# A second seven-product level in layer 3's second matrix, and layer 0's row vector fetched from DRAM, in a four-layer graph kernel on one core

## The chip, the core and the metric

The kernel runs on one core of one Trainium2 chip, in one launch. The metric is the device time in microseconds (us) of that launch; the figure of the kernel before is the median of three runs. All data are 32-bit floats. In the profile PE is TensorE's multiplying side and PEld its weight loads, DVE is VectorE, ACT is ScalarE, POOL is GpSimd, and SP is the engine whose queue issues nearly all DMA transfers. One matrix multiplication of the program shows in the profile as two weight loads and two MATMUL records (a transposition shows as one of each).

## The reference, cut to what matters

There are 128 graphs of 64 nodes with 512 features: `x` is 128x64x512, `adj` is 128x64x64. Four layers follow each other, each of the form x = layernorm(x + layer(x)). Layer 0 and layer 3 are what the change touches:

```python
# layer 0
s = (x @ w) @ a
A = tanh((s[..., :, None] + s[..., None, :]) / 8.0) * 8.0
A = exp(where(A >= 0, A, 0.1 * A)) * adj
A = A / sum(A, axis=-1) * sum(adj, axis=-1)
out = A @ x @ w
# layer 3: x 512 wide, W1 1024x512, W2 512x1024; H = (adj != 0)
h = layer_norm(relu(hypergraph_conv(x, adj, W1, b1)), gamma, beta)
y = hypergraph_conv(h, adj, W2, b2) + x
# hypergraph_conv(x, adj, W, b) = Dn * (H @ (Be * (H.T @ (x @ W.T)))) + b
```

Layer 1 has three 512x512 matrices (two of them are multiplied together beforehand), layer 2 likewise.

## The kernel before, in words

**Tiling.** Two graphs share the 128 partitions, which makes 64 tiles of 128 tokens. A group is two tiles (`GT` = 2, `TOK` = 256 tokens), so there are 32 groups; two groups (`SG` = 2) are a pair and go through the layers together. The first and the last pair (`APART_3A`) are the exception: their four groups run one by one. So 14 calls of `run` handle a pair and 4 handle a single group. `run` records every layer's operations for its groups.

**Seven products.** Every large matrix is applied by a seven-product scheme: the left side is cut into 2x2 blocks ("11" to "22") with four sums of them (`side_sums`), the matrix into four blocks and three combinations (`combine`), and seven products of blocks replace eight. `pair_products` does this for a pair (512 tokens). The seven matrix pieces come from DRAM: `stored_in_place` and `stored_twice` store them once at the start, and `streamed` loads them for each call into the eight buffers of kind "ring", 512 KB a load (1024 floats a partition).

**Layer 3's first matrix ("3a")** already goes one level further for pairs: `forty_nine_products` treats each of the seven products as seven again. `inner_sums` makes four sums on DVE for the left side, `inner_products` issues seven products into two PSUM banks, and `into` carries them out of PSUM, three steps on ACT and three on DVE for each of the seven sets. DVE (and twice POOL) then adds the seven results in `use`.

**Layer 3's second matrix ("3b")** before is one level: `pair_products(a, s_, streamed("3b"), ..., chunks=KH // 2)`. That is 7 products x 2 token halves x 4 chunks, 56 multiplications of 128x128 by 128x256 for a pair. Each product is added into `x` by DVE straight from PSUM with the node scale (`pair_scaled_into`), 14 instructions for a pair.

**Layer 0's row vector.** `row_dot` makes s for a tile as a column, one value a partition. Tanh needs it as rows as well: ACT writes the column times an identity (`diag`), and `over_graph(diag, ps_s)` multiplies that with the block matrix of ones `same` on PE, so that s stands in PSUM along the free axis in all partitions of its graph; ACT reads it from there. `over_graph` is used twice more for each group, for row sums in layers 0 and 2.

**What sets the order.** `run` executes nothing itself: each step adds operations to `Order`, with the engine, a planned cost (`w_pe`, `w_dve`, `w_act`, `w_pool`) and a key. `Order.run` lists them by planned times, gives out buffers (`kinds`: 17 "k4", 8 "ring", 7 "x" and so on) and emits them; every engine then keeps that order strictly. Keys come from the fitted tables `BASE` (one number for each group), `EARLY`, `LEAD` and `PREPARED`. PE has "whole" operations (all 128x128 cells) and divided ones ("quarters" and "columns", which use 64 rows or columns and run side by side); `choose` plans a cost (`TURN`) for going from one to the other. `over_graph` may be either. DVE operations that read no PSUM, and all of POOL's, are marked `port` and planned so that they do not overlap.

Of the kernel before, what the change touches and what calls it, by code (L numbers as in the profile page):

```python
# [16 lines left out]
P = 128  # L17
B, N, D, DH = 128, 64, 512, 1024
T = B * N // P
GT = 2  # L20
# [8 lines left out]
APART = 4  # L29

BASE = [
    6.0035, 8.2772, 13.2033, 17.6332, 26.0202, 27.1146, 41.4888, 43.61,
    52.2405, 53.0756, 62.4617, 70.5981, 77.7498, 79.4232, 91.2587, 95.4559,
    102.4733, 106.2595, 111.4315, 119.1324, 126.0769, 128.4967, 140.1767, 144.9507,
    152.9702, 154.7354, 165.7456, 173.1973, 169.6391, 182.4004, 188.4128, 191.0087,
]
RESIDENT = ("m1", "m2")
APART_3A = (0, NG // SG - 1)
LEAD = [37.2697, 5.5754]
PREPARED = [28.6382, 16.68, 12.9121, 14.55, 17.8769, 0.587]  # L40
PIECE = 1024
EPS = 1e-5
TINY = 1.1754944e-38
# [26 lines left out]
class Order:  # L70
    LATENCY = {"PE": 210, "DVE": 125, "ACT": 140, "POOL": 120, "SP": 3500}
    AGAIN = {"PE": 0, "DVE": 115, "ACT": 115, "POOL": 120}
    TO_PE = 50
    BYTES_PER_NS = 260
    UNDERWAY = 8
    TURN, TURN_DIVIDED = 110, 60

    NEAR = 27.7595
    FAR = 251.4563
    ENOUGH = 0.0205  # L80

    EARLY = [14.4537, -21.4408, 7.6077, 25.6747, 2.625, 1.3768, 16.3015, 8.7929, -1.7454, 13.9409, 11.8891, -1.629, 2.9263, -2.9931, 14.9219, -6.7676]

    BLOCK = 64
    REST = 4500
    AHEAD = 15.591
    TOGETHER = 0.0013
    OLDEST = 1000000000.0
    SPARE = {"k4": 0, "ring": 1}

    def __init__(self, slots):
        self.slots = {kind: list(range(n))[::-1] for kind, n in slots.items()}
# [204 lines left out]
def kernel(  # L297
# [34 lines left out]
    def kind(name, n, *shape, space=None):  # L332
        kinds[name] = [(space or sbuf).tile([P, *shape], FP, name=f"{name}{i}") for i in range(n)]

    kind("x", 7, GT, D)
    kind("k4", 17, PIECE)
    kind("ring", 8, PIECE)
    kind("h", 2, GT, DH)
    kind("k2", 2, D)
    kind("adj", 6, CT, N)  # L340
    kind("kept", 6, CT, N)
    kind("bh", 2, CT, N + 2)
    kind("e", 4, GT, N)
    kind("col", 28, 16)
    kind("bank", 8, D, space=psum)
    kinds["product"] = [None] * 3
# [357 lines left out]
                made[f"b{h + 1}{i + 1}"] = (q, lambda q=q: rows_of(q, cols // 2))  # L704
        return made

    def stored_twice(which, w):

        stored_in_place(which + "1", quarters(w), PIECE, PIECE)
        width = w.shape[1] // 4  # L710
        store = in_dram(which, width, [k + "." + j for k in USE for j in USE])
        for n, (k, (src, _)) in enumerate(zip(USE, stored[which + "1"])):
            order.key = PREPARED[4] + PREPARED[5] * n
            q = Buf("k4", 4)
            order.add("SP", 500, [src, in_turn], [q], lambda q=q, src=src: nc.sync.dma_start(out=q.t, in_=src.t), size=P * PIECE * 4)
            view = lambda q=q: rows_of(q, 2 * width)
            b = {f"b{h + 1}{i + 1}": (q[2 * h + i], lambda view=view, h=h, i=i: view()[:, h : h + 1, ts(1 - i, width)])
                 for h in range(2) for i in range(2)}
            for j in USE:
                if j[0] == "b":  # L720
                    store(k + "." + j, b[j])
            t = {"t1": b["b11"], "t3": b["b12"], "t2": b["b22"], "t4": b["b21"]}
            combine(b, t, width)
            for j in USE:
                if j[0] == "t":
                    store(k + "." + j, t[j])

    order.key = PREPARED[2]
    stored_twice("3a", w3a)


    order.key = PREPARED[3]
# [9 lines left out]
    for k, (q, view) in w3b_q.items():  # L742
        for c in range(KH // 2):
            row = (int(k[1]) - 1) * (KH // 2) + c
            act(D // 2, [gamma_c, q], [q], lambda view=view, c=c, row=row: nc.scalar.activation(
                view()[:, c, :], view()[:, c, :], AF.Identity, scale=gamma_c.t[:, row : row + 1]))
    stored_in_place("3b", w3b_q, PIECE, PIECE)

    def streamed(which, room=()):

        pieces = []
        chunks = {"3a": 1, "3b": KH // 2}.get(which, KC // 2)
        for src, n in stored[which]:
            width = PIECE // src.cells
            t_ = Buf("ring")
            order.add("SP", 500, [src[list(range(n))]], [t_, *(room if not pieces else ())],
                      lambda t_=t_, src=src, n=n, width=width: nc.sync.dma_start(
                          out=t_.t[:, : n * width], in_=src.t[:, : n * width]),
                      urgent=1.5, size=P * n * width * 4)
            if pieces:  # L760
                order.ops[-1].led = lead
            else:
                lead = order.ops[-1]
            for k in range(n):
                pieces.append((t_, lambda t_=t_, k=k, width=width: t_.t[:, ts(k, width)].rearrange(
                    "p (c o) -> p c o", c=chunks)))
        return pieces
# [294 lines left out]
        return room, at  # L1062


    def inner_products(raw, room, at, which, pieces, f, width):


        going, x_, y_ = Buf("inner"), Buf("bank"), Buf("bank")
        raw_tok, raw_view = raw

        def side(k):
            if k in KEYS:
                return raw_tok, lambda: raw_view(k)
            return room[int(k)], lambda: at(int(k))[:, which]

        def times(bank, i, k, start=True):
            piece, view = next(pieces)
            token, left = side(k)

            def emit():  # L1080
                nc.tensor.matmul(bank.t[:, ts(i, width)], left(), view()[:, 0], start=start, stop=True, skip_group_check=True)

            pe(w_pe(width), [token, piece, going], [bank, *([y_] if k == "11" else [])], emit, matmuls=1)

        def into(cells, bank, i, n=1, first=False):
            n *= width
            dst = lambda: f.t[:, cells[0] * width : cells[0] * width + n]
            src = lambda: bank.t[:, i * width : i * width + n]
            if first:
                act(n, [bank], [f[cells]], lambda: nc.scalar.copy(dst(), src()), NOW)  # L1090
            else:
                dve(n, [bank, f[cells]], [f[cells]], lambda: nc.vector.tensor_add(dst(), src(), dst()), NOW)

        times(x_, 1, "11")
        times(x_, 0, "0", False)
        into([1, 2], x_, 0, 2, True)
        times(y_, 0, "12")
        times(x_, 1, "1", False)
        times(x_, 0, "3", False)
        into([0], x_, 1, 1, True)  # L1100
        into([0], x_, 0)
        into([2], y_, 0)
        times(x_, 1, "2", False)
        into([1], x_, 1)
        times(x_, 1, "22", False)
        into([3], x_, 1, 1, True)
# [198 lines left out]
    def run(groups):  # L1305
# [27 lines left out]
        for g in groups:  # L1333
            step(0, g)
            xt, own = xt_[g], own_[g]
            adj, turned, gm, am, sums, g1, dc, dh = prepared[g // GC]
            s, diag, e, ps_s = Buf("col", GT), Buf("e", GT), Buf("e", GT), Buf("bank")
            for t in range(GT):
                row_dot([xt[[2 * t, 2 * t + 1]], u0_b], s[t], lambda t=t, xt=xt: xt.t[:, t, :], lambda: u0_b.t)
                act(N + 40, [s[t]], [diag[t]], lambda t=t, s=s, diag=diag: nc.scalar.activation(  # L1340
                    diag.t[:, t], eye, AF.Identity, scale=s.t[:, t : t + 1]))

            over_graph(diag, ps_s)
            for t in range(GT):
                act(N + 40, [ps_s, s[t]], [e[t]], lambda t=t, s=s, e=e, ps_s=ps_s: nc.scalar.activation(
                    e.t[:, t], tiles(ps_s)[:, t], AF.Tanh, bias=s.t[:, t : t + 1]), NOW)
            dve(GT * N, [e], [e], lambda e=e: nc.vector.scalar_tensor_tensor(e.t, e.t, 0.1, e.t, ALU.mult, ALU.max))
            act(GT * N, [e], [e], lambda e=e: nc.scalar.activation(e.t, e.t, AF.Exp, scale=8.0))
            dve(GT * N, [e, adj], [e], lambda e=e, adj=adj, own=own: nc.vector.tensor_mul(e.t, e.t, adj.t[:, own]))

            ps_e, rs = Buf("bank"), Buf("e")
            over_graph(e, ps_e)
            dve(7 * GT * N, [ps_e], [rs], lambda rs=rs, ps_e=ps_e: nc.vector.reciprocal(flat(rs.t), ps_e.t[:, : GT * N]), NOW)
            dve(GT * N, [e, rs], [e], lambda e=e, rs=rs: nc.vector.tensor_mul(e.t, e.t, rs.t))
            step(1, g)
            gT0.append(gathered(*of_x[g], lambda h, t, e=e: e.t[halves[h][0], t, :], [e]))
            scales.append((sums, 2 * CT + own.start))
# [204 lines left out]
        step(15)  # L1562
        sx = {g: Buf("col", 2 * GT) for g in groups}
        if n == SG:
            pair_products(a, s_, streamed("3b"), *pair_scaled_into([xt_[g] for g in groups], scales, [sx[g] for g in groups]), chunks=KH // 2)
        else:
            g, (f, at) = groups[0], scales[0]
            seven_products({**a, "deep": True}, s_, streamed("3b"), *scaled_into(at_x[g], f, slice(at, at + GT), D // 2, sx[g]))
        for g in groups:
            step(15, g if n == 1 else last_of)  # L1570
            xt = xt_[g]
# [101 lines left out]
```

## Time and profile before

| | |
|---|---|
| median of three runs | 2114.53 us (2114.24 to 2114.62) |
| the profiled execution's own time | 2114.4 us |
| its span, first to last instruction | 2112.6 us |
| granted TensorE clock | 0.999 |
| PE / PEld busy | 2097.3 (99%) / 1773.1 us (84%) |
| DVE busy | 1361.7 us (64%), 3768 instructions |
| ACT busy | 1168.2 us (55%), 2538 instructions |
| POOL busy | 458.3 us (22%), 434 instructions |
| DMA | 345.00 MB, mean 163 GB/s |

The span leaves out 1.8 us of the execution's own time. Nearly every instruction has one line number (L1602 before, L1654 after), that of the function that records the emitted instruction, so groups are told apart by the names of the buffers: `bank<-ring,k` is a multiplication into a PSUM bank with one operand from a "ring" buffer (a streamed matrix piece) and one from a "k" buffer. A group line ends with the busy time, the mean duration of one in ns, and the idle time of the engine just before these instructions with what ended it. MATMUL records overlap each other (a new one starts while the last one drains), so their mean duration is not what one costs; the distance from start to start is.

### The profile page before, as it was taken

How to read it: one execution, taken by the hardware profiler on the slowest of the kernel's cores; microseconds unless marked ns; L12 is line 12 of the kernel's file. 1: busy time of each engine (PE TensorE's matmuls, PEld its weight loads, DVE VectorE, ACT ScalarE, POOL GpSimd, SP SyncE). 2: the span in 40 equal slices, each digit the busy share in tenths (PEclk: the TensorE clock that was granted, in tenths of full speed). 3: DMA queues.
4: the chain of work that ended last, by engine and by line, in shares of the span. 5: the costliest groups of instructions: out<-in, count | busy, mean ns of one | idle time of the engine just before them, and what ended most of it. 6: DMA issues, size and time to landing. Idle time of an engine off the chain costs nothing.

```text
span 2112.6 us, 49594 instructions
## 1 busy us (share of the span) xinstructions
PE 2097.3 (99%) x19867; PEld 1773.1 (84%) x19867; DVE 1361.7 (64%) x3768; ACT 1168.2 (55%) x2538; POOL 458.3 (22%) x434
## 2 busy tenths in 40 slices
PE   8999999999999999999999999999999999999998
PEld 4887788888888888888888888888888888888876
DVE  5765668765677547676585664866667665675644
ACT  3445655663555546664555664647447465374555
POOL 1121230411214013130131311222121221222120
PEclk9999999999999999999999999999999999999999
DMA  8677674533436236262352533435434454253655
GB/s 293 214 259 260 242 239 153 188 139 123 143 120 223 80 113 208 94 223 102 113 179 92 198 121 106 165 123 183 140 103 156 137 191 140 80 186 120 208 175 200
DMA packets 142102, 345.00 MB, mean 163 GB/s; under 512 B 32240, under 2 KB 49840, under 8 KB 141872
## 3 DMA queue, kind: packets, MB, share of 16 engines
q1 hardware_dynamic: 141872, 341.83, 47.4%
q8 instruction: 157, 2.57, 0.5%
q14 instruction: 73, 0.60, 0.1%
HBM read 305.70 MB, written 36.08 MB: 162 GB/s over the span
## 4 chain that ended last, share of the span: by engine, by line
PE 98%; ACT 1%; DMA 0%; DVE 0%; issue 0%; SPq 0%; POOL 0%; POOLq 0%; ACTq 0%; DVEq 0%
PE bank L1602 98%; ACT k L1602 1%; DMA k<-in_wk_dram 0%; DVE e L1602 0%; ACT x L1602 0%; SPq L1602 0%; ACT e L1602 0%; ACT m L1602 0%; DVE col L1602 0%; DVE k L1602 0%; POOL col L1602 0%; DVE m L1602 0%; POOLq L1669 0%; DVE x L1602 0%; ACT bw_b L1602 0%
## 5 line engine op out<-in xcount | busy, mean ns | idle before, releaser
L1602 PE MATMUL bank<-ring,k 128*128 128x256 f32 (+1 forms) x4940 | 1178.3, 387 | 0.3 <-ACT k L1602 0.3
L1602 PEld LDWEIGHTS bank<-ring,k 128*128 128x128 f32 x4940 | 916.8, 190 | 146.8 <-issue 24.5
L1602 ACT COPY k<-bank 128x512 f32<-128x512 f32 (+1 forms) x822 | 406.7, 529 | 368.0 <-PE bank L1602 365.0
L1602 DVE SCALAR_TENSOR_TENSOR x<-bank,col,x 128x256 f32<-128x256 f32 (+1 forms) x736 | 341.3, 503 | 218.6 <-PE bank L1602 204.8
L1602 PE MATMUL bank<-k,m 128*128 128x256 f32 (+1 forms) x2016 | 426.7, 358 | 0.7 <-ACT k L1602 0.7
L1602 PEld LDWEIGHTS bank<-k,m 128*128 128x128 f32 x2016 | 347.4, 190 | 43.9 <-issue 1.9
L1602 POOL TENSOR_TENSOR col<-col,mhalf 128x2 f32<-128x2 f32 (+1 forms) x161 | 111.8, 695 | 1007.0 <-DVE col L1602 750.9
L1602 DVE TENSOR_TENSOR k<-bank,k 128x256 f32<-128x256 f32 (+1 forms) x456 | 216.2, 494 | 158.4 <-PE bank L1602 107.4
L1602 ACT ACTIVATE k<-x,col 128x512 f32<-128x512 f32 x256 | 183.6, 720 | 187.8 <-DVE col L1602 160.7
L1602 PE MATMUL bank<-ring,h 128*128 128x256 f32 x1024 | 238.2, 380 | 0.0
L1602 ACT ACTIVATE x<-x,col,col 128x512 f32<-128x512 f32 x256 | 199.0, 814 | 53.1 <-DVE col L1602 52.9
L1602 PEld LDWEIGHTS bank<-ring,h 128*128 128x128 f32 x1024 | 192.7, 190 | 27.1 <-issue 0.9
L1602 DVE TENSOR_TENSOR k<-k,k 128x512 f32<-128x512 f32 (+3 forms) x319 | 191.6, 617 | 4.0 <-ACT k L1602 3.7
L1602 DVE TENSOR_TENSOR k<-k 128x256 f32<-128x256 f32 (+2 forms) x223 | 113.9, 526 | 61.7 <-ACT k L1602 53.5
L1602 DVE TENSOR_SCALAR col<-col 128x2 f32<-128x2 f32 (+2 forms) x402 | 73.8, 193 | 86.2 <-ACT k L1602 75.2
L1602 DVE TENSOR_TENSOR h<-k,k 128x1024 f32<-128x1024 f32 (+1 forms) x88 | 105.7, 1208 | 18.3 <-ACT k L1602 18.1
L1602 POOL TENSOR_TENSOR k<-k,k 128x1024 f32<-128x1024 f32 (+1 forms) x31 | 72.1, 2326 | 182.0 <-DVE h L1602 65.9
L1602 PE MATMUL bank<-k,k 128*64 128x64 f32 (+1 forms) x2112 | 104.1, 237 | 5.5 <-DMA k<-in_wk_dram 5.5
L1602 POOL TENSOR_TENSOR k<-k,b3b_b 128x512 f32<-128x512 f32 x64 | 82.3, 1293 | 116.3 <-ACT k L1602 51.7
L1602 PEld LDWEIGHTS bank<-k,k 128*64 128x64 f32 (+1 forms) x2112 | 77.0, 139 | 33.8 <-issue 20.4
L1602 POOL TENSOR_TENSOR x<-x,bv_b 128x512 f32<-128x512 f32 x64 | 81.3, 1279 | 106.2 <-ACT k L1602 34.2
L1602 ACT ACTIVATE k<-bank,u_c 128x256 f32<-128x256 f32 (+1 forms) x144 | 59.9, 445 | 65.2 <-PE bank L1602 65.1
(103 smaller groups left out, 1624.4 us busy)
## 6 DMA issues: line engine op xcount, KB each, us to landing
ring<-3a SPq DMA_DIRECT2D x196, 512.0 KB, 4.3
ring<-3b SPq DMA_DIRECT2D x126, 512.0 KB, 4.3
ring<-v SPq DMA_DIRECT2D x105, 512.0 KB, 4.4
ring<-w SPq DMA_DIRECT2D x51, 512.0 KB, 4.9
x<-in_x_dram SPq DMA_DIRECT2D x32, 512.0 KB, 5.2
out_dram<-x SPq DMA_DIRECT2D x31, 512.0 KB, 4.7
ring<-v SPq DMA_DIRECT2D x35, 256.0 KB, 4.4
3a<-k SPq DMA_DIRECT2D x49, 128.0 KB, 3.8
```

What stands on the lines that cost most here:

```text
L1602: made = f(*args, **kwargs)
```

## The change

1. **3b for pairs becomes 49 products.** `run` calls `inner_sums` and `inner_products` for each of the seven outer products, with two chunks each (`parts=2`) and a result width of 128 columns: 7 x 7 x 2 = 98 multiplications of 128x128 by 128x128. Seven sets of results go to SBUF buffers of kind "k2", are added there (`sum_of`, five times on DVE and twice on POOL for a pair), and reach `x` by 8 DVE instructions that now read SBUF (`into_x`).
2. **Its pieces.** `stored_twice` becomes `stored_inner`, called for "3a" as before and for "3b" too: seven stored pieces are loaded again, combined (21 DVE and 7 POOL instructions in all) and stored as 49 pieces of 128 KB. A pair streams 13 loads (6.4 MB) where it streamed seven (3.7 MB). The four single groups keep the seven pieces, now called "3b1".
3. **s as rows.** For groups from the third on, `diag` and its `over_graph` go. The column is stored to DRAM (one DMA of 4-byte elements) and loaded back as rows, once for each half of the partitions; tanh reads SBUF. The first two groups keep the old way.
4. **Tables and buffers.** `BASE`, `LEAD`, `PREPARED`, `EARLY` and the planner's constants get other values; "x" goes from 7 buffers to 6, "k4" from 17 to 15, "bh" from 2 to 1, "k2" from 2 to 8 and "e" from 4 to 6. So the whole list of every engine is ordered anew.

```diff
-    TO_PE = 50
-    BYTES_PER_NS = 260
-    UNDERWAY = 8
+    TO_PE = 100
+    BYTES_PER_NS = 290
+    UNDERWAY = 6
...
-    stored_in_place("3b", w3b_q, PIECE, PIECE)
+    stored_in_place("3b1", w3b_q, PIECE, PIECE)
+    stored_inner("3b", D // 4, 2, PREPARED[3] + PREPARED[6], PREPARED[5])
...
-    def inner_products(raw, room, at, which, pieces, f, width):
+    def inner_products(raw, room, at, which, pieces, f, width, parts=1):
...
             def emit():
-                nc.tensor.matmul(bank.t[:, ts(i, width)], left(), view()[:, 0], start=start, stop=True, skip_group_check=True)
-
-            pe(w_pe(width), [token, piece, going], [bank, *([y_] if k == "11" else [])], emit, matmuls=1)
+                for c in range(parts):
+                    nc.tensor.matmul(bank.t[:, ts(i, width)], left() if parts == 1 else left()[:, c], view()[:, c],
+                                     start=start and c == 0, stop=c == parts - 1, skip_group_check=True)
+
+            pe(w_pe(width, parts), [token, piece, going], [bank, *([y_] if k == "11" else [])], emit, matmuls=parts)
...
-                act(N + 40, [s[t]], [diag[t]], lambda t=t, s=s, diag=diag: nc.scalar.activation(
-                    diag.t[:, t], eye, AF.Identity, scale=s.t[:, t : t + 1]))
-
-            over_graph(diag, ps_s)
+            if g < SG:
...
+                over_graph(diag, s_row)
+                rows_of_s = lambda s_row=s_row: tiles(s_row)
+            else:
+                s_row, kept_s = Buf("e", 2), const(dram.tile([GT * P], FP, name=f"s_{g}"))
+                dma(P * 64, [s], [kept_s], lambda kept_s=kept_s: kept_s.t.rearrange("(t p) -> p t", p=P), lambda s=s: s.t[:, :GT])
+                for h, (rows, _) in enumerate(halves):
+                    src = kept_s.t.rearrange("(t h i) -> h t i", h=2, i=N)[h]
+                    dma(P * GT * N * 2, [kept_s], [s_row[h]], lambda rows=rows, s_row=s_row: s_row.t[rows],
+                        lambda src=src: bass.AP(tensor=src.tensor, offset=src.offset, ap=[[0, N], *src.ap]))
...
-            pair_products(a, s_, streamed("3b"), *pair_scaled_into([xt_[g] for g in groups], scales, [sx[g] for g in groups]), chunks=KH // 2)
+            outer_of = {"1": a["11"], "2": a["12"], "4": a["22"], "5": s_[0], "6": s_[1], "7": s_[2], "3": s_[3]}
+            pieces, kept_3b = iter(streamed("3b")), {}
...
+            for name in ("1", "5", "2", "6", "3", "7", "4"):
+                token, view = outer_of[name]
+                blocks = {k: (lambda k=k, view=view: view()[:, ts(col(k), 2), ts(row(k), P)]) for k in KEYS}
+                room, at_room = inner_sums({"tokens": token, **blocks}, (P, 2))
+                f = Buf("k2", 4)
+                inner_products((token, lambda k, blocks=blocks: blocks[k]()), room, at_room, 0, pieces, f, P, 2)
+                if name == "2":
+                    into_x(0, 0, sum_of(kept_3b["1"], f, out=f))
...
+                elif name == "4":
+                    into_x(1, 0, sum_of(kept_3b["7"], f, out=f))
+                kept_3b[name] = f
```

## The prediction

> **What bounds the kernel now.** I read the page's busy line first, then the chain that ended last.
>
> ```profile
> PE 2097.3 (99%) x19867; PEld 1773.1 (84%) x19867; DVE 1361.7 (64%) x3768; ACT 1168.2 (55%) x2538; POOL 458.3 (22%) x434
> PE 98%; ACT 1%; DMA 0%; DVE 0%; issue 0%; SPq 0%; POOL 0%; POOLq 0%; ACTq 0%; DVEq 0%
> ```
>
> PE never rests, and the chain is PE itself. So the time is the sum of the distances from one matmul's start to the next. The timeline of PE gives them: subtract the start of a row from that of the next and divide by its count.
>
> ```profile
> 59.24 1.95 PE L1602 MATMUL bank<-k,m 128*128 128x128 f32 x16
> 61.02 3.62 PE L1602 MATMUL bank<-ring,k 128*128 128x256 f32 x16
> 64.48 0.49 PE L1602 MATMUL bank<-e,same 128*128 128x128 f32 x2
> ```
>
> A record 128 columns wide costs 1.78/16 = 0.111 us, one of 256 costs 3.46/16 = 0.216 us. Half the columns cost 51%. The third view is the timeline where PE goes from whole to divided operations and back.
>
> ```profile
> 348.71 1.89 PE L1602 MATMUL bank<-ring,k 128*128 128x256 f32 x8
> 350.53 1.63 PE L1602 MATMUL bank<-kept,h 64*64 64x64 f32 x96
> 352.08 3.72 PE L1602 MATMUL bank<-ring,k 128*128 128x256 f32 x16
> 355.74 0.69 PE L1602 MATMUL bank<-kept,h 64*64 64x64 f32 x32
> 356.25 1.11 PE L1602 MATMUL bank<-e,x 64*64 64x64 f32 x64
> ...
> 2092.73 0.69 PE L1602 MATMUL bank<-kept,h 64*64 64x64 f32 x32
> 2093.36 1.99 PE L1602 MATMUL bank<-ring,k 128*128 128x256 f32 x8
> ```
>
> The x8 row takes 1.82 us, 0.09 over 8 x 0.216, because a divided row follows; the x16 row takes 3.66, 0.20 over, because it stands between two. The 32 divided records take 0.51 us when divided ones follow and 0.63 when a whole one does. One excursion into divided work thus costs 0.09 + 0.11 + 0.12 = 0.32 us beside the work itself.
>
> The last view, groups kept apart by shape, has the prices for the other engines; the stretch line shows their load in the steady part, with PE unbroken.
>
> ```profile
> L1602 DVE SCALAR_TENSOR_TENSOR x<-bank,col,x 128x256 f32<-128x256 f32 x672 | 297.0, 480 | 201.7 <-PE bank L1602 188.2 <-ACT k L1602 5.5 <-POOL k L1602 2.7
> L1602 DVE TENSOR_TENSOR k<-k,k 128x512 f32<-128x512 f32 x169 | 119.5, 729 | 3.9 <-ACT k L1602 3.7
> L1602 DVE TENSOR_TENSOR k<-k 128x256 f32<-128x256 f32 x137 | 58.1, 443 | 22.1 <-ACT k L1602 18.1 <-POOL k L1602 2.3 <-PE bank L1602 1.4
> L1602 DVE TENSOR_TENSOR k<-k,k 128x256 f32<-128x256 f32 x116 | 56.8, 498 | 0.1
> L1602 DVE DVE_READ_ACCUMULATOR x<-bank,col,x 128x1 f32 x448 | 37.0, 83 | 0.0
> L1602 DVE TENSOR_TENSOR e<-bank,kept 128x128 f32<-128x128 f32 x32 | 9.3, 289 | 20.3 <-PE bank L1602 19.4 <-ACT h L1602 0.5
> 264.00:1980.00 1716.00, 1716.00 (x16425) 1476.69 (x16425) 1122.19 (x3100) 962.78 (x2088) 380.15 (x353) 1.00 0.43 147
> ```
>
> **The change part by part.** The sum is made against the profiled execution: 2114.4 us, of which 2112.6 are span; the median, 2114.53, stands 0.1 above it, which I ignore.
>
> *3b on PE.* A pair loses 56 multiplications of 256 columns, 112 records, 24.2 us, and gets 98 of 128 columns, 196 records, 21.8 us. Over 14 pairs: 338.7 - 304.6 = **34.1 us saved**. All of it lies on the path. Lower bound: at 0.112, which a run of 11 such records nearby shows, 31.4.
>
> A rule of the Trainium skill speaks against this step. The page "TensorE: Matmul & The Clock Gate", section "Back-to-back issue gap", says that in a stream where every matmul has its own weight load the spacing is set by both, and gives about 81 ns for 128 columns where the matmul alone would need 56, a factor of 1.45. By that the 2744 new records would cost 137 us more and the change would be a loss of about 100 us. The x16 row is such a stream, each record with its own 128-column load, and shows no such surcharge; I go by the row.
>
> *s as rows on PE.* By the emitted order 31 whole `over_graph` calls go: 62 records x 0.111 = **6.9 us saved**; ACT loses 60 diagonals of 0.34 us.
>
> *The new order on PE.* Counting the runs in the emitted lists, PE enters divided work 165 times before and 197 times after, with the same divided work. 32 x 0.32 = **10.2 us lost**. Bounds: 32 x 0.20 (the whole side alone) = 6.4, and 12.
>
> *DVE.* A pair gets 28 block sums of 256 (0.45 each, the mean of the two 256 rows), 21 additions of 128 from PSUM (0.29), five of 512 (0.71) and eight scaled additions of 256 with accumulator (0.44 + 0.08): 12.6 + 6.1 + 3.5 + 4.2 = 26.4 us. It loses 14 scaled additions, eight with accumulator: 6.8 us. Times 14, and 21 preparation instructions of 0.45: +284 us, to 1646 us, 79% of the new span. ACT gets 42 us net of copies by 98 sets x (0.37 + 2 x 0.27) = 89 less 20: about 1237 us, 59%. POOL gets 28 additions of 512 at 1.28 and 7 of 0.73: +41, to 499 us. None of this is on the path as long as PE has other work. But PE now waits inside each set: the products go in two banks, and the fourth, sixth and seventh product need ACT's and DVE's removal first. Before, seven sets a pair had three such round trips; now fourteen have, and on DVE whatever is queued ahead (a 1024-wide addition takes 1.2 us) delays all later PSUM removals, and with them PE. In the steady part of before DVE idles 35% and PE waits nowhere (1716.00 of 1716.00); afterwards DVE idles 21%. Bounds for new waits: 0, and, were 3b's DVE work confined to 3b's own PE time, (26.4 - 21.8) x 14 = 64 us. By the emitted order 3b's products come mostly in runs of 2 to 16 with other stages' work between them, so I am near the low end: **8 us lost**.
>
> *DMA and SP.* Pairs stream 38.5 MB more, preparation reads 3.7 and writes 6.4 MB more: 345 to about 394 MB, 189 GB/s; the page's slices reach 293. SP issues 1076 transfers for 847, about 0.4 us each, hidden. The store of s and the two loads wait on SP for `row_dot` and for the store's landing, and behind them queue the ring loads. The nearest rows, loads of rows from DRAM (`adj<-mask_rows`, 4.5 us to landing) and the store `mask_rows<-e` (4.4), make the way 9 us where ACT, PE and ACT took about 1. That is hidden by the rest of a pair's 131 us; uncovered it would cost up to 8 us a pair, 112 in all. I take 0.
>
> *The end.* Before, the last group's normalization is split by tile: from the last PE end (2105.9) to the end of the span pass 6.7 us, with two stores of 256 KB landing in 2.0. In the emitted order after, group 30 ends last, unsplit: scaled addition 0.56, column work 0.31, two squares with accumulators 1.82, column work and POOL's power 1.02, two scalings 1.6, about 0.6 of handovers, and a store of 512 KB, 0.4 to issue and between 2.0 and 4.4 to land. 8.3 to 10.7 us, so **3 us lost**. The start keeps its order of loads: 0.
>
> Sum: -34.1 - 6.9 + 10.2 + 8 + 3 = -19.8; 2114.4 - 19.8 = 2094.6, forecast **2095 us**.
>
> **Rivals.** What separates no change from a change here is 0.2%, 4.2 us: faster is below 2110.3, slower above 2118.8.
>
> *No new waits.* Excursions at 6.4 and no waits: 2114.4 - 34.1 - 6.9 + 6.4 + 1.6 = 2081. For it: PE waits nowhere in the steady part. Against: DVE's idle share falls by two fifths.
>
> *DVE becomes the bound inside 3b.* Without waits the sum is 2086.6; it is slower than before from 32 us of waits on, half of the 64. For it: DVE's work for a set, 26.4/7 = 3.8 us, exceeds PE's 3.1, and the 3a sets before them are dense too. With 45 us of waits: 2132. Against: the interleaving in the emitted order, and that 79% leaves room over a pair.
>
> *The saving is just eaten.* Waits of 24 to 32 us, by the same mechanism or by the ring loads coming late behind the s transfers: 2114.
>
> **How the numbers follow.** Forecast case (waits of 2 to 24 us) 0.62, no new waits 0.15, just eaten 0.07, DVE-bound 0.16. Faster 0.77, same 0.07, slower 0.16. The range goes from 2078 (the no-wait case with 128-column records at 0.110) to 2124, which leaves out the worse half of the slower case.
>
> **What the profile after would show.** `bank<-ring,k` and `bank<-ring,h` groups of 128x128, 2744 records together, in timeline runs of 0.111 us each; a pitch near 0.16 would break the first step. `bank<-e,same` falls by about 60 records. DVE near 1650 us. In the waits of PE, DVE `k` and ACT `k` should sum to a few us, in the stretches in mid-run PE should stay over 99%; if DVE's row there is over 90% while PE's is under 97%, the DVE rival holds. PE waiting for `ring<-3b` would mean late loads. The last store would be a single 512 KB one, some 9 us after the last matmul.

## The result, and the profile after

The changed kernel takes 2245.8 us (median of four runs, 2239.0 to 2248.8) against 2114.51 for the kernel before in the same session: a ratio of 1.0616, with a 95% interval from 1.0596 to 1.0637. It is 131 us slower, and the range of the forecast ended at 2124. The profiled execution took 2245.1 us, of which 2243.2 are span.

The page's busy line and the chain that ended last, by engine and by line:

```profile
PE 2125.0 (95%) x20985; PEld 1804.4 (80%) x20985; DVE 1554.5 (69%) x4460; ACT 1230.7 (55%) x2772; POOL 501.7 (22%) x469
PE 61%; DMA 10%; ACT 4%; DVE 3%; issue 1%; SPq 1%; POOL 0%; ACTq 0%; POOLq 0%; DVEq 0%
PE bank L1654 61%; DMA s<-col 5%; DMA e<-s 4%; ACT k L1654 2%; DVE k L1654 2%; DVE h L1654 1%; ACT h L1654 1%; DMA ring<-3a 1%; DMA ring<-3b 1%; SPq L1654 1%; ACT x L1654 1%; ACT e L1654 0%; DVE col L1654 0%; DVE x L1654 0%; POOL col L1654 0%
```

PE was 98% of the chain and is 61%. Two transfers that did not exist before, the store of s (`s<-col`) and its loads as rows (`e<-s`), hold 8.2% (4.5 and 3.7 before rounding). The steady stretch (columns: window, us, busy time and count for PE, PEld, DVE, ACT and POOL, granted clock, DMA share, GB/s) says how far PE is from unbroken work:

```profile
264.00:1990.00 1726.00, 1639.85 (x16457) 1414.29 (x16456) 1230.07 (x3505) 966.38 (x2172) 404.90 (x371) 0.98 0.51 163
```

86 us of the 1726 are without PE, and DVE is at 71%, less loaded than forecast. The list of waits (total us, times, longest) tells for whom PE stands, and who stands for s. `DVE e` is the end of the chain that starts with s: tanh and exp on ACT, then DVE, then PE.

```profile
SPq L1654 <- DMA s<-col: 161.9, 27, 8.4
ACT e L1654 <- DMA e<-s: 105.0, 24, 12.9
PE bank L1654 <- ACT k L1654: 32.5, 22, 5.2
PE bank L1654 <- DVE e L1654: 26.0, 10, 8.5
```

SP, which issues nearly all transfers, stands 161.9 us for the landing of `s<-col`, with everything queued behind. The DMA issue lists (count, KB each, median us to landing) give what the forecast had taken as 4.4 and 4.5:

```profile
s<-col SPq DMA_DIRECT2D x30, 1.0 KB, 8.2
e<-s SPq DMA_DIRECT2D x60, 32.0 KB, 3.5
```

The smallest transfer of the kernel, 1 KB, takes longer to land than any other that recurs through it (`x` follows with 5.7). One place shows the damage, first in the chain (start, us, what), then in the timeline of PE:

```profile
567.41 8.33 DMA s<-col
576.51 10.43 DMA e<-s
```

```profile
579.38 1.03 PE L1654 MATMUL bank<-k,m 128*128 128x256 f32 x4
588.90 0.80 PE L1654 MATMUL bank<-e,same 128*128 128x128 f32 x2 [8.49 <-DVE e L1654]
589.49 1.91 PE L1654 MATMUL bank<-ring,k 128*128 128x256 f32 x4
591.20 3.73 PE L1654 MATMUL bank<-k,m 128*128 128x256 f32 x12
```

From the issue of the store to the landing of the rows it takes 19.5 us (567.41 to 586.94). PE runs out of work at 580.4 and stands 8.5 us, the last two of them after the rows have landed, with ACT and DVE between them and PE. Afterwards four records of 256 columns take 1.71 us, 0.43 each, twice the 0.216 of before. The stretches around it show both reasons (the pair's second store went out at 577.2):

```profile
580.00:588.00 8.00, 0.41 (x2) 0.01 (x1) 0.37 (x3) 0.99 (x4) 0.00 (x0) 0.68 0.97 61
588.00:592.00 4.00, 3.10 (x8) 2.62 (x9) 1.91 (x8) 3.19 (x10) 0.70 (x1) 0.50 0.25 91
```

In the gap the DMA engines count as 97% busy and move 61 GB/s; behind it the granted clock is 0.50. By the clock records of the whole trace, 15 stretches of 3.4 to 10 us before the end, some 82 us together, ran at 0.5, which cost PE about 21 us on its whole records (they stand among the waits in the table below).

**Where PE's time went.** With the distance from one start to the next, as in the prediction, the span falls into five parts: whole records at their pitch (0.111 and 0.216 us; 0.429 at 512 columns), what lies between whole records beyond that (waits), the edges of an excursion into divided work (entering, leaving, the first record after), the inside of divided work, and what lies before the first and after the last start. The kernels "no store" and "no store, no side work" are experiments told below (`x6_no_store`, `x11_no_3b_sums_no_removal`).

| us | before | after | no store | no store, no side work |
|---|---|---|---|---|
| whole records at pitch | 1812.5 | 1771.5 | 1771.5 | 1771.5 |
| waits between them | 8.1 | 119.2 | 41.5 | 31.6 |
| edges of excursions (how many) | 61.7 (166) | 105.1 (198) | 84.6 (198) | 83.9 (198) |
| inside divided work | 219.1 | 233.8 | 219.7 | 219.2 |
| start and end | 11.2 | 13.6 | 13.5 | 13.6 |
| span | 2112.6 | 2243.2 | 2130.8 | 2119.8 |

The first row falls by 41.0, what the prediction saved on PE (34.1 + 6.9). It is a count times these pitches, so it confirms the counts alone; the pitches themselves are looked at below. All the loss lies in the other rows.

### The profile page after: what moved, and what is told of

It is laid out like the page before. It is cut to its first block, busy times and chain, and to the rows that moved or that the text cites. A ratio compares the mean times of both kernels' runs of the same rounds, so it can differ in the third digit from the quotient of the medians.

```text
span 2243.2 us, 53522 instructions
## 1 busy us (share of the span) xinstructions
PE 2125.0 (95%) x20985; PEld 1804.4 (80%) x20985; DVE 1554.5 (69%) x4460; ACT 1230.7 (55%) x2772; POOL 501.7 (22%) x469
## 4 chain that ended last, share of the span: by engine, by line
PE 61%; DMA 10%; ACT 4%; DVE 3%; issue 1%; SPq 1%; POOL 0%; ACTq 0%; POOLq 0%; DVEq 0%
PE bank L1654 61%; DMA s<-col 5%; DMA e<-s 4%; ACT k L1654 2%; DVE k L1654 2%; DVE h L1654 1%; ACT h L1654 1%; DMA ring<-3a 1%; DMA ring<-3b 1%; SPq L1654 1%; ACT x L1654 1%; ACT e L1654 0%; DVE col L1654 0%; DVE x L1654 0%; POOL col L1654 0%
## 5 line engine op out<-in xcount | busy, mean ns | idle before, releaser
L1654 PE MATMUL bank<-ring,k 128*128 128x256 f32 (+1 forms) x6340 | 1316.8, 356 | 38.4 <-ACT k L1654 20.2
L1654 PEld LDWEIGHTS bank<-ring,k 128*128 128x128 f32 x6340 | 1047.6, 193 | 193.9 <-issue 37.0
L1654 ACT COPY k<-bank 128x512 f32<-128x512 f32 (+2 forms) x1116 | 493.4, 469 | 548.5 <-PE bank L1654 523.3
L1654 DVE TENSOR_TENSOR k<-bank,k 128x256 f32<-128x256 f32 (+2 forms) x750 | 297.0, 413 | 187.4 <-PE bank L1654 106.5
L1654 DVE SCALAR_TENSOR_TENSOR x<-bank,col,x 128x256 f32<-128x256 f32 (+1 forms) x540 | 255.8, 512 | 106.6 <-PE bank L1654 98.7
L1654 DVE TENSOR_TENSOR k<-k,k 128x512 f32<-128x512 f32 (+3 forms) x473 | 268.1, 583 | 9.8 <-ACT k L1654 8.2
L1654 DVE TENSOR_TENSOR k<-k 128x256 f32<-128x256 f32 (+2 forms) x328 | 152.3, 478 | 32.2 <-ACT k L1654 21.8
L1654 POOL TENSOR_TENSOR k<-k,k 128x1024 f32<-128x1024 f32 (+1 forms) x59 | 107.9, 1829 | 189.3 <-ACT k L1654 107.6
L1654 PE MATMUL bank<-ring,h 128*128 128x128 f32 (+1 forms) x800 | 130.2, 295 | 0.8 <-DVE k L1654 0.5
L1654 PEld LDWEIGHTS bank<-ring,h 128*128 128x128 f32 x800 | 112.3, 193 | 5.8 <-DVE k L1654 0.7
```

What stands on the lines that cost most here:

```text
L1654: made = f(*args, **kwargs)
```

## The experiments

Two theories at first: that the round trip of s by way of DRAM is late and its readers wait (the 19.5 us above), or that 3b's denser side work on DVE and ACT makes PE wait. The first three kernels take the waits for s apart.

**Nobody waits for s.** Store and loads are issued at their places, the loads read rows that exist from the start, and tanh reads a constant tile.

```diff
-                    src = kept_s.t.rearrange("(t h i) -> h t i", h=2, i=N)[h]
+                    src = mask_rows.t[g * TOK : (g + 1) * TOK].rearrange("(t h i) -> h t i", h=2, i=N)[h]
...
-                rows_of_s = lambda s_row=s_row: s_row.t
+                rows_of_s = lambda: same.rearrange("p (t i) -> p t i", i=N)
```

> Everything of the changed kernel in the same order on every engine, but nothing waits for s from DRAM: the store of s is still issued, the two loads read a constant DRAM tensor (the mask's rows) and so do not wait for the store, and tanh reads a constant SBUF tile instead of the loaded rows, so s rows are left out of the result. Theory 1 (the way of s through DRAM costs the time): what is left is the forecast's sum without it, 2085 to 2110 us. Theory 2 (DVE is the bound inside the 49 products): 2200 us or more, PE still waiting for ACT k and DVE k. In between, 2130 to 2180, would mean both.

Measured: 2215.1 us, ratio 1.0473 (1.0434 to 1.0513). Only 31 of the 131 us went, though no load and no tanh waits for s any more (SP's list still puts 19.9 us down to the store's landing, where it had 161.9). As a matter of waiting for s the first theory fell. The time lies in the range that the second was given, but the kernels below show another cause.

**Only SP's wait for the store taken out**: the first of the two edits alone, so tanh still waits for its loads.

> The changed kernel in the same order, the store of s still issued, but its two loads read a constant DRAM tensor, so SP does not wait for the store to land (8.2 us median); tanh still waits for the loads. s is replaced by the mask in the result. Theory 1a (SP's 162 us of waiting for the store is the larger part, and holds up the ring loads behind it): 2100 to 2140 us. Theory 1b (the latency of the loads alone is enough, because ACT stands before tanh): 2180 to 2230. Theory 2 (DVE): no change, 2240.

Measured: 2240.8 us, ratio 1.0595 (1.0484 to 1.0705; two executions, 20 us apart), nearly all of the loss. The loads, no longer held until the store has landed, now take longer themselves:

```profile
e<-mask_rows SPq DMA_DIRECT2D x60, 32.0 KB, 9.8
```

9.8 us instead of 3.5: whether the wait stands at SP or in the DMA queues, what comes after the store arrives late.

**The same store in 128 pieces of 8 bytes** instead of 256 of 4, with the loads and tanh reading that order (a load then takes 512 bytes in one piece for a partition, not two of 256).

```diff
-                dma(P * 64, [s], [kept_s], lambda kept_s=kept_s: kept_s.t.rearrange("(t p) -> p t", p=P), lambda s=s: s.t[:, :GT])
+                dma(P * 64, [s], [kept_s], lambda kept_s=kept_s: kept_s.t.rearrange("(p t) -> p t", p=P), lambda s=s: s.t[:, :GT])
...
```

> The changed kernel with the same values and the same order, but the two values of s of a partition stand side by side in DRAM: the store writes 128 pieces of 8 bytes instead of 256 of 4, and each load reads 512 bytes in one piece for a partition instead of two of 256. Theory 1: the landing of the store depends on the number of pieces, falls from 8.2 us to about 5, and the time falls by a third of the loss, to about 2200 us. If landing does not depend on the pieces: 2245. Theory 2: 2245.

Measured: 2145.5 us, ratio 1.0144 (1.0115 to 1.0174). 100 of the 131 us hang on how 1 KB is cut up, more than the third that was expected. The store lands in 5.3 us instead of 8.2.

**s by way of DRAM without 3b's 49 products**: the kernel before with part 3 of the change and before's tables, so newly ordered by the same planner; and the same with the 8-byte store.

> The kernel before with its own tables and one-level second matrix; only s of the groups from the third on goes through DRAM (the planner makes its order anew with its assumption of 3.5 us for a landing). Theory 1: slower than before although PE has 31 whole multiplications less: 2150 to 2220 us, with ACT waiting for e<-s and SP for s<-col. Theory 2: about 2108 us, 7 us faster.

> The kernel before with s of the groups from the third on through DRAM, as in the run that took 2255 us, in that run's order, but with s stored in 128 pieces of 8 bytes and loaded in pieces of 512. Theory 1': the store's pieces are nearly all of that loss, so 2115 to 2150 us; the latency theory (the way through DRAM is too long in any layout): above 2200.

Measured: 2255.2 us, ratio 1.0663 (1.0606 to 1.072), and 2130.4, ratio 1.0079 (1.0058 to 1.0099); the first is above the 2220 at which its range ended. The layout of the store alone is worth 125 us here, and the loss needs nothing of 3b. Even cut into 8 bytes, s as rows does not pay in this order: the whole records fall by the 6.9 us, the edges rise by 15.7 with 38 excursions more, the waits by 6.3.

**The store itself, which nobody waits for, in the kernel before.** 30 stores of 1 KB go out with the loads of `x`, with a place in DRAM of their own that nobody reads; everything else is the kernel before, in its order. Four cuts, one line of code for each: 256 pieces of 4 bytes side by side, 128 of 8, 256 of 4 bytes 512 bytes apart, and the same 64 bytes apart.

```diff
+            nc.sync.dma_start(out=spare.rearrange("(t p) -> p t", p=P), in_=mhalf)
+            nc.sync.dma_start(out=spare.rearrange("(p t) -> p t", p=P), in_=mhalf)
+            nc.sync.dma_start(out=spare.rearrange("(t p o) -> p t o", p=P, o=128)[:, :, 0], in_=mhalf)
+            nc.sync.dma_start(out=spare.rearrange("(t p o) -> p t o", p=P, o=16)[:, :, 0], in_=mhalf)
```

> The kernel before with its own order, and 30 stores more that nobody waits for: just ahead of each load of x from the third group on, SP stores a constant 128x2 tile to DRAM in 256 pieces of 4 bytes that lie in one KB, the layout that the change uses for s. Theory 1': slower than before by 60 to 140 us, although no instruction waits for these stores. Rival (the harm is in waiting for the store, not in its traffic): within 5 us of before.

> As the kernel before with 30 unread stores, but with the two values of a partition side by side: 128 pieces of 8 bytes in one KB. Theory 1': the harm goes with the number of pieces, so half or less of that of the 4-byte stores. If it goes with the bytes or the number of stores: the same.

> As the kernel before with 30 unread stores of 256 pieces of 4 bytes, but every piece 512 bytes from the next (128 KB in all). If the pieces' lying in one KB is what makes them slow (they hit the same DRAM place one after another): within 10 us of before. If small pieces are slow wherever they lie: as slow as the packed 4-byte stores.

> Kernel before with 30 stores that nobody reads, 256 pieces of 4 bytes each, now 64 bytes apart in DRAM (packed side by side they cost 51 us, 512 bytes apart 0.6 us). If what collides is pieces that fall into one stretch of 512 bytes, it is as dear as packed, about 2165 us. If the stretch is 64 bytes or less, it is free, about 2115 us. A value between would mean a stretch of 128 or 256 bytes.

| 30 unread stores of 1 KB | us | ratio to before | store lands, us | loads of `x` behind it land, us |
|---|---|---|---|---|
| 4 bytes, side by side | 2165.0 | 1.0241 (1.022 to 1.0261) | 10.7 | 11.0 |
| 8 bytes, side by side | 2116.0 | 1.0009 (0.9999 to 1.0019) | 5.4 | 7.0 |
| 4 bytes, 64 apart | 2114.6 | 0.9999 (0.999 to 1.0009) | 4.0 | 5.1 |
| 4 bytes, 512 apart | 2114.5 | 1.0002 (0.9992 to 1.0013) | 4.1 | 4.9 |

In the kernel before, without such a store, the loads of `x` land in 5.2 us.

The issue lists of the first and of the 64-byte one, from which the last two columns are:

```profile
x<-in_x_dram SPq DMA_DIRECT2D x32, 512.0 KB, 11.0
...
spare<-mhalf SPq DMA_DIRECT2D x30, 1.0 KB, 10.7
```

```profile
x<-in_x_dram SPq DMA_DIRECT2D x32, 512.0 KB, 5.1
...
spare<-mhalf SPq DMA_DIRECT2D x30, 1.0 KB, 4.0
```

Neither the bytes nor the number of pieces costs anything by itself: 256 pieces of 4 bytes are free as soon as they lie 64 bytes apart. Side by side they cost 51 us in a kernel in which nothing reads them. So the price is paid by the other transfers, and the packet times of the traces show it. Of the packets of 512 bytes and more, 135 took over 3 us beside the 4-byte store (the longest 8.2), 23 beside the 8-byte store, and none with the pieces 64 or 512 bytes apart or in the kernel before. The changed kernel also has 135 of them, 40 with the 8-byte store, and none without the store (the last of these kernels follows below). In the changed kernel the jam can be seen around one store, issued at 465.99, first in the timeline of SP's queue, then by stretches:

```profile
465.99 0.37 SPq L1654 DMA_DIRECT2D s<-col  x1
466.41 0.93 SPq L1654 DMA_DIRECT2D ring<-3b  x2
467.38 0.61 SPq L1654 DMA_DIRECT2D adj<-in_adjT_dram  x1
468.66 0.33 SPq L1654 DMA_DIRECT2D ring<-3b  x1
469.03 0.43 SPq L1654 DMA_DIRECT2D x<-in_x_dram  x1
474.22 1.95 SPq L1654 DMA_DIRECT2D e<-s  x2
```

```profile
462.00:467.00 5.00, 5.00 (x25) 4.41 (x24) 5.00 (x12) 2.31 (x6) 2.42 (x2) 1.00 0.63 213
468.50:475.50 7.00, 7.00 (x34) 6.17 (x33) 7.00 (x7) 3.94 (x8) 0.00 (x0) 1.00 0.80 74
475.50:482.00 6.50, 6.50 (x32) 5.72 (x31) 3.35 (x7) 3.32 (x8) 0.62 (x1) 1.00 0.89 307
```

Three loads to `ring`, one to `adj` and one to `x` are issued right behind the store. For 7 us the DMA engines are 80% busy and move 74 GB/s; then the jam is over, and they move 307. Stores differ: in the kernel with the 30 unread 4-byte stores the same 7 us (2.5 to 9.5 after the issue) carry 81 GB/s in the median, from 27 to 317, and 178 with the pieces 64 bytes apart.

The page "DMA: Bandwidth & Descriptors" of the Trainium skill, section "Specifications", asks for at least 512 bytes in a transfer for full rate, since below that the DMA engine reads, modifies and writes. The runs narrow that: 4-byte pieces 64 bytes apart, each far under 512, cost nothing that can be measured, while 4-byte neighbours cost 2.4% and 8-byte neighbours at most 0.19%. Why neighbours are dear stays open: no run here looks inside the engine.

**The change without the store.** The order of after, every instruction at its place, but the 30 stores left out; the loads read the rows of masks, and tanh waits for them.

```diff
-                dma(P * 64, [s], [kept_s], lambda kept_s=kept_s: kept_s.t.rearrange("(t p) -> p t", p=P), lambda s=s: s.t[:, :GT])
+                order.add("SP", 500, [s], [kept_s], lambda: None, size=P * 64)
```

> The changed kernel in the same order on every engine, with the 30 stores of s left out; the loads of rows read a constant DRAM tensor (the mask's rows, so s rows are left out of the result), and tanh waits for them as before. Theory 1' (after the first four runs: each store of 256 four-byte pieces into one KB slows every DMA transfer behind it for some 8 us, so ring loads and row loads come late): 2085 to 2110 us, row loads landing in 4 to 5 us, under 20 us of PE waits. Theory 2 (the 49 products load DVE so that PE waits): still above 2130.

Measured: 2132.6 us, ratio 1.0087 (1.007 to 1.0104), above the 2085 to 2110 that were expected of the transfers alone. The store is worth 113 of the 131 us; against the kernel with only SP's wait taken out, whose loads are the same, it is about 108. The remaining 18 us belong to the order and to 3b: the profiled span is 2130.8 and PE is 92% of the chain again (98% before), but it waits in many small places, where before it had waits of 8.7 us in all.

```profile
PE bank L1654 <- ACT k L1654: 8.4, 11, 1.9
PE bank L1654 <- DVE k L1654: 7.5, 13, 1.2
PE bank L1654 <- ACT x L1654: 5.7, 7, 2.9
```

(Another 6.0 us are the wait for the first loads, `k<-in_wk_dram`, 5.5 before.) The next three kernels start from this one. **The loads of the rows are not waited for:** tanh reads a constant tile.

> The kernel without the stores of s, in the same order, whose 60 loads of rows are still issued but tanh reads a constant tile, so that nothing waits for them. If the loads' latency still costs anything in the 2132.57 us: below 2125. If the plan covers 4 to 5 us of landing: 2129 to 2134.

Measured: 2133.6 us, ratio 1.0093 (1.0078 to 1.0108), no difference: without the store the loads' way is hidden, as forecast. **3b's 392 block sums on DVE left out** (`inner_sums` emits nothing for 3b):

```diff
-                at(i), left(), right()))
+                at(i), left(), right()) if emitted else None)
```

> The kernel without the stores of s (2132.57 us, which leaves out the s rows), in the same order, and besides without the 392 block sums on DVE ahead of 3b's products (their results are left out). DVE has about 170 us less to do, while every product still waits for the removal of the one before it from PSUM. Theory 3 (DVE's load is what is left of the loss: PE waits because DVE is behind): 2100 to 2112 us. Theory 4 (what is left is the round trips from PE through ACT and DVE inside a set, whatever DVE's load): 2122 to 2132.

Measured: 2127.7 us, ratio 1.0067 (1.005 to 1.0083): 5 us. **3b's products are not taken out of PSUM** for pairs (the buffers keep zeros), so the fourth, sixth and seventh product of a set wait for nobody:

```diff
-                act(n, [bank], [f[cells]], lambda: nc.scalar.copy(dst(), src()), NOW)
+                act(n, [bank], [f[cells]], lambda: nc.scalar.copy(dst(), src()) if parts == 1 else None, NOW)
...
-                dve(n, [bank, f[cells]], [f[cells]], lambda: nc.vector.tensor_add(dst(), src(), dst()), NOW)
+                dve(n, [bank, f[cells]], [f[cells]], lambda: nc.vector.tensor_add(dst(), src(), dst()) if parts == 1 else None, NOW)
```

> The kernel without the stores of s, in the same order, with the block sums but without the removal of 3b's products from PSUM (294 copies on ACT, 294 additions on DVE; the results are left out). No product of a 3b set waits for one before it, and DVE has only 80 us less to do. Theory 4 (round trips): 2095 to 2112 us. Theory 3 (DVE's load): 2118 to 2130.

Measured: 2122.7 us, ratio 1.0044 (1.0029 to 1.0059): 10 us. The first of these two results lies in the range that was expected if round trips through PSUM were the cause, the second in the range for DVE's load, so neither is the whole cause. **Both left out:**

> The order of after with the 30 stores of s left out, and with both the 392 block sums of 3b on DVE and the removal of 3b's products from PSUM for pairs left out (the kernels that leave out one of the two took 2127.7 and 2122.7 us, against 2132.6 with both). If the remaining waits of PE come from 3b's side work, the two savings add up and more: at or below 2118 us, PE's stalls (42.6 us with both) under 25 us. If they come from how the list is ordered around other stages (transpositions waiting for ACT, loads, the two extra trips a pair into divided work), little more goes than with the dearer one alone: 2121 us or more, stalls about 32 us.

Measured: 2121.2 us, ratio 1.0032 (1.0019 to 1.0045). Together they are worth 11 us, hardly more than the dearer one. DVE does as much in this kernel as before the change (1373.7 us), and PE still waits:

```profile
PE bank L1656 <- ACT k L1656: 7.3, 8, 1.9
PE bank L1656 <- DMA ring<-3b: 6.6, 5, 2.6
PE bank L1656 <- ACT x L1656: 3.6, 5, 2.6
```

The waits for DVE `k` are down from 7.5 to 1.9 us, those for ACT `k` only from 8.4 to 7.3, and the loads of 3b's pieces come late instead (6.6 for 2.4). By the table, 23.5 us of waits over before are left (31.6 against 8.1). They stay without 3b's side work, so they are put down to the new list itself and its loads: transpositions waiting for `x`, products 256 and 512 columns wide (not 3b's) waiting for ACT, loads of 3b's pieces, 13 for a pair instead of seven. Which of the new tables' values puts each there was not tried, and stays open. No kernel that was run is faster than the one before.

## Why the prediction was wrong, step by step

**Right: PE's saving.** The counts fell as forecast, and the pitches held. In the kernel without the store the 128-column records stand 0.111 us apart when nothing interrupts them (8 in 0.89 us):

```profile
739.31 1.05 PE L1654 MATMUL bank<-ring,k 128*128 128x128 f32 x8
740.20 1.03 PE L1654 MATMUL bank<-k,m 128*128 128x256 f32 x4
```

The row of before held, and the surcharge of 1.45 for their own weight loads, which the prediction set against it, appears nowhere: the median pitch of 3b's records after is 0.112 us.

**Right: the excursions, the end, the engines' load in the main.** The typical edges are 0.093 for entering, 0.149 for leaving and 0.104 for the record after, in every kernel of the table; 32 excursions more (198 for 166) at 0.346 make 11.1 us where 10.2 were forecast. The measured edges rise by more, which is taken up below. Start and end cost 2.4 us more, forecast 3. ACT, POOL and DMA came within 1% of the forecast (1231, 502 us, 396 MB). (The "42 us net" in its passage on ACT is no term of its sum: 89 less 20 on 1168 gives the 1237.) DVE stands at 1555 us, not 1646: summed by group its work rose by 246 us, not 284 (the 256-wide sums took 0.41 to 0.42 us each, not 0.45), and as its records overlap each other more, its busy time rose by 193.

**Failed: "DMA and SP", where the text says "I take 0".** The price of the store came from the nearest rows, `mask_rows<-e` (4.4 us) and `adj<-mask_rows` (4.5), and was treated as a latency that the rest of a pair hides. Where no such store jams the queues that held: without it nobody feels the loads (2132.6 and 2133.6). With it, waiting for s is worth 31 us, and the other 100 are lost with nobody waiting. What the step left out is that a transfer can cost time to those queued with it. The store `mask_rows<-e` writes 64 rows of 512 bytes; the new one has 256 pieces of 4 bytes next to each other, which neither row resembles. The description of the change names the 4-byte elements; the step passed over them. Cost: 113 us, of which 78 are more waits between whole records (the half clock included), 20 longer edges and 14 inside divided work. The upper bound in the prediction, "8 us a pair, 112 in all", fits the figure by chance: it was meant for the way of s when nothing hides it, and without any wait for s 100 us of the loss remain.

**Mis-sized: the waits inside 3b; missing: the waits elsewhere in the new order.** 8 us were taken of a range from 0 to 64, for 3b alone; "The new order on PE" counted excursions and put no waits beside them. Without the store, waits rose by 33.4 us, of which by the distances of starts 16.0 stand directly ahead of 3b's own products and 17.4 ahead of others; the edges rose beyond the 11.1 above by another 11.8. Together that is 45. With 45 for 8 the prediction's sum gives 2094.6 + 37 = 2132, and 2132.6 is measured; this is the bookkeeping of the table again and proves no cause. So the loss without the store stands where the DVE rival stood (2132 with 45 us of waits), by chance and not by its mechanism: its test was DVE over 90% in the stretches where PE is under 97%. Of 14 stretches of 120 us in mid-run only this one has PE under 97% (95%), and DVE stands at 83%:

```profile
300.00:420.00 120.00, 114.11 (x1166) 97.18 (x1165) 99.48 (x296) 69.20 (x157) 29.36 (x30) 1.00 0.76 246
```

Leaving out the sums, 128 us of DVE's work, won 5 us. PSUM's round trips are worth 10, both together 11. The rest fits a list that no longer has spare work ready at every point, but what puts each wait there is not shown. That the emitted order shows other work between 3b's products was true and did not suffice.

The chances followed from these two steps: the 0.16 for slower knew one mechanism, DVE in 3b. Late ring loads behind the transfers of s stood only in the "just eaten" rival, with 0.07 and 24 to 32 us.

## What to carry to other kernels

A transfer is not priced by its bytes and its landing alone: look at how it is cut on the DRAM side, and ask what it does to the transfers queued with it. A row vector that leaves SBUF as one element a partition should go out with its pieces apart, or with more bytes in each, before anyone counts what it saves on PE. The pieces 64 bytes apart were run only as a store that nobody reads, and with pieces of 8 bytes s as rows still lost 0.8% in the kernel before. And where PE has no gap in a hand-ordered list, a new order's small waits are a term of the sum of the size of the saving (45 against 41 us here), which the list of operations does not show.

## What the runs showed of the hardware that was not expected

A store of 1 KB in 256 pieces of 4 bytes side by side slows what is queued with it, at the place shown for about 7 us (213 GB/s ahead of it, 74 behind it, 307 afterwards), and takes 8.2 to 10.7 us to land in the median; 64 bytes apart it lands in 4.0 and costs nothing measurable (ratio 0.9999, 0.999 to 1.0009). With 8 bytes a piece it costs at most 0.19% where nobody reads it. In the changed kernel, where s is read, 13 us over the kernel without the store remain (2145.5 against 2132.6).

A pause of PE of 8.5 us is followed by 0.50 of the clock, and records of 256 columns 0.43 us apart, so that wait is paid twice. In the trace of the changed kernel nine pauses of PE exceed 3 us; eight are followed by a stretch at 0.50, one of 3.7 us is not, and the other seven such stretches follow pauses of 1.6 to 2.9 us. The page "TensorE: Matmul & The Clock Gate" of the Trainium skill, section "Part 1: The HAM clock gate (the "warmup" mystery)", says that the clock is halved after an idle window of about 3.4 us and comes back after one of steady work. The 8.5 us pause agrees; the shorter pauses ahead of other stretches do not show that threshold (the ends of PE's records are modelled).
